# Program order for SyncE's DMA queue in layers 1 to 3 of a four-layer graph-attention kernel

## The chip, the cores and the metric

The kernel runs on one core of a Trainium2 chip. The metric is the device time of one execution in microseconds (us). The core's engines work side by side, each with its own list of instructions: TensorE (PE in the profile; PEld are its weight loads), VectorE (DVE), ScalarE (ACT), GpSimd (POOL) and SyncE (SP). In this kernel SyncE issues the plain transfers between the core's memories and DRAM, and POOL issues the indirect ones, which gather rows by index. A program writes its instructions once, in one sequence; a scheduler then gives each engine its order, and semaphores hold an instruction until what it needs is there.

## What is computed

Four graph-attention layers over 4096 nodes with 256 features, all with the same adjacency matrix (about one entry in 256 set, and the diagonal). Each ends in a residual and a layer norm:

```python
# layers 0 and 1: 4 heads of 64; layer 2: 2 heads of 128, separate weights for source, target and value
h   = x @ W
e   = leaky_relu(src[:, None] + dst[None, :], 0.2)     # one number per node on each side, per head
att = softmax(where(adj, e, -inf), axis=1)
x   = layernorm(x + att @ h)
# layer 3: one head, softmax of e and of -e, both over x, then a product and elu
hp  = concat([att(e) @ x, -att(-e) @ x], axis=1)
x   = layernorm(x + elu(hp @ fc_W))
```

In layer 2 the softmax runs over the other axis of a transposed score, which is the same form. `fc_W` is multiplied in ahead of the attention, so layer 3 gathers two blocks of 256 values per node.

## The kernel before

**Lists.** While layer 0 runs, the kernel turns the adjacency matrix into packed neighbour lists. The 4096 nodes are 32 row tiles of 128. For each row tile the columns that have an entry are packed into 13 groups (`NG`) of 128 gathered rows; with the tile's own 128 rows that makes 14 positions (`NP`). Groups 0 to 5 (`FRONT`) hold nodes of the first 17 row blocks (`MIX`) alone; groups 6 to 12 may hold any node. (A dense version stands behind a flag, for other matrices; it doesn't run here.)

**One row tile** (`RowTile`) has two halves of seven positions: half 0 is groups 0 to 5 and the own rows, half 1 is groups 6 to 12. `load` issues, for half 0, the edge terms `S` and the mask `mk` on SyncE; for half 1, the residual input `y` on SyncE; then for each position a gather `G` from the layer's `vals` on POOL (L629), or for the own rows a plain load `G` on SyncE (L626). `half` makes the attention weights `w` on ScalarE and VectorE (L670 and L666 to L671; in layer 3 L657 to L660) and multiplies them on PE (L679 in layer 1, L682 in layers 2 and 3). `finish` divides by the softmax's sum, adds `y` and normalizes (`norm`); the row goes to `xp` in DRAM, or in layer 3 to `out`.

**Projection of a finished row** (`Projection`): transpose (L532), copy `xT` on ScalarE (L537), products with the next layer's weights (L546), the row of `vals` on VectorE (L572), its store on SyncE (L574), then the edge terms (L578 to L585). So row m of the next layer's `vals` can exist a few steps after tile m of this layer is done. A gather of groups 0 to 5 of the next layer waits for `vals` rows 0 to 16, and one of groups 6 to 12 for all 32.

**Whole rows.** In layer 2 the last three blocks of four row tiles, and in layer 3 the last block, aren't gathered: `whole_rows` multiplies them densely, with loads of `Sw`, `mw` and `vw` on SyncE (L874, L886, L888) and products on PE (L911). These pieces are spread over the half steps of the other tiles.

**The order of the program.** A layer goes in half steps `part(m, 0)` and `part(m, 1)`. A part 0 first asks for the loads of tiles m and m + 1 that aren't yet asked for. Then come the half's products, the pieces of a projection of an earlier row, and the finish of tile m - 1. `close` goes from one layer to the next: it writes the rest of this layer's work, mixed with the first halves of tiles 0 and 1 of the next. In `norm` the store of a finished row stands right behind the last operation on it:

```python
        for i, (y, m) in enumerate(self.group):
            nc.vector.tensor_scalar(y, y, mv[:, i, 0:1], r[:, i:i + 1], op0=ALU.subtract, op1=ALU.mult)
            dst = self.prog.out if self.n == 3 else self.shared["x"][self.n + 1]
            nc.sync.dma_start(out=dst[m * P:(m + 1) * P, :], in_=y)          # L958
```

This written order isn't that of the queue: the scheduler may put a load far ahead of where it is written, once its buffer is free. Buffers are rotating pools: 4 of `S` and `mk`, 9 of `y`, 16 slots for `G` (a slot holds two positions in layers 1 and 2, one in layer 3) and 14 more for half 1 of layer 3.

Of the kernel before, what the change touches and what calls it, by code (L numbers as in the profile page):

```python
# [37 lines left out]
F32 = mybir.dt.float32  # L38
# [12 lines left out]
P = 128  # L51
# [78 lines left out]
def to_tiles(ap):  # L130
    return ap.rearrange("(t p) f -> p t f", p=P)
# [55 lines left out]
class Program:  # L187
# [24 lines left out]

    def weights(self, n):

        nc, ins, H = self.nc, self.ins, HEADS[n]
        V = F if n < 3 else 2 * F
        wext = self.wpool.tile([P, KT, 2 * F + 4 * H4], F32, name="wext")
        ablks, nats, brow = [], [], None
        if n < 2:
            nc.sync.dma_start(out=wext[:, :, :F], in_=to_tiles(ins[f"W{n}T"]))  # L220
            for k, a in enumerate(("src", "dst")):
                ablk = self.small.tile([P, KT, H4], F32, name=f"ablk{k}")
                nc.vector.memset(ablk, 0.0)
                for h in range(H4):
                    r = slice((h % 2) * D4, (h % 2) * D4 + D4)
                    vec = ins["a0s" if k == 0 else "a0d"][h] if n == 0 else ins["a1"][h, k * D4:(k + 1) * D4]
                    load_vec(nc, ablk[r, h // 2, h:h + 1], vec)
                ablks.append(ablk)
                nats.append(ins[f"W{n}"])
        elif n == 2:  # L230
            nc.sync.dma_start(out=wext[:, :, :F], in_=to_tiles(ins["W23T"]))
            for k in range(2):
                ablk = self.small.tile([P, KT, 2], F32, name=f"ablk{k}")
                nc.vector.memset(ablk, 0.0)
                for h in range(2):
                    load_vec(nc, ablk[:, h, h:h + 1], ins["a2"][h, k * P:(k + 1) * P])
                ablks.append(ablk)
                nats.append(ins["W21" if k == 0 else "W22"])
            brow = self.small.tile([1, F + 3 * H], F32, name="brow")
            nc.sync.dma_start(out=brow[:, :F], in_=ins["b23"].rearrange("(o f) -> o f", o=1))  # L240
            ones = self.small.tile([1, P], F32, name="ones")
            nc.vector.memset(ones, 1.0)
            self.ones = ones
        else:
            fc = to_tiles(ins["fc3"])
            for k in range(2):
                nc.sync.dma_start(out=wext[:, :, k * F:(k + 1) * F], in_=fc[:, k * KT:(k + 1) * KT, :])
                ablk = self.small.tile([P, KT, 1], F32, name=f"ablk{k}")
                for q in range(KT):
                    load_vec(nc, ablk[:, q, 0:1], ins["a3"][(k * KT + q) * P:(k * KT + q + 1) * P])  # L250
                ablks.append(ablk)
                nats.append(ins["W3T"])

        T = TERMS[n]

        def scaled(dst, src, k):

            nc.vector.tensor_scalar(dst[:, k * T:(k + 1) * T], src, SLOPE, None, op0=ALU.mult)
            if k == 1:
                nc.vector.tensor_scalar(dst[:, 2 * T:3 * T], src, NEG_SLOPE, None, op0=ALU.mult)  # L260
                if n == 3:
                    nc.vector.tensor_scalar(dst[:, 3 * T:4 * T], src, -NEG_SLOPE, None, op0=ALU.mult)

        for k in range(2):
            nat = self.io.tile([P, KT, F], F32, name="nat")
            nc.sync.dma_start(out=nat, in_=to_tiles(nats[k]))
            for m in range(KT):
                pw = self.bank(self.banks)
                for q in range(KT):
                    nc.tensor.matmul(pw[:, :T], nat[:, q, m * P:(m + 1) * P], ablks[k][:, q, :],  # L270
                                     start=(q == 0), stop=(q == KT - 1))
                scaled(wext[:, m, V:], pw[:, :T], k)
            if n == 2:
                bcol = self.small.tile([P, KT], F32, name=f"bcol{k}")
                for q in range(KT):
                    load_vec(nc, bcol[:, q:q + 1], ins["b21" if k == 0 else "b22"][q * P:(q + 1) * P])
                pb = self.bank(self.banks)
                for q in range(KT):
                    nc.tensor.matmul(pb[:1, :T], bcol[:, q:q + 1], ablks[k][:, q, :],
                                     start=(q == 0), stop=(q == KT - 1))  # L280
                scaled(brow[:, V:], pb[:1, :T], k)
        return wext, brow


    def lists(self, ctx):
# [191 lines left out]

    def run(self):
        ins, nc = self.ins, self.nc
        w0 = self.weights(0)  # L480
        layer = Layer(self, 0)
        with ExitStack() as ctx:
            lists = self.lists(ctx)
            xs = []
            for q in range(NT // 2):
                slot = self.g0.tile([P, 2 * ROW[0]], F32, name="G")
                nc.sync.dma_start(out=slot[:, :2 * F].rearrange("p (t f) -> p t f", t=2),
                                  in_=to_tiles(ins["x"][2 * q * P:2 * (q + 1) * P, :]))
                xs += [slot[:, :F], slot[:, F:2 * F]]

            line = [Projection(self, 0, w0, x, m, (self.ptwo[0], self.ptwo[1], self.pfour))
                    for m, x in enumerate(xs)]
            turns, listed = NT + 5, 0
            for m in range(turns):
                while listed < BT + LEAD and listed * turns <= m * (BT + LEAD):
                    next(lists)
                    listed += 1
                for k, step in enumerate(Projection.STEPS):
                    if 0 <= m - k < NT:
                        step(line[m - k])  # L500

            for m in range(NT):
                layer.part(m, 0)
                if m + LEAD < NT:
                    next(lists)
                layer.part(m, 1)
            for _ in lists:
                pass
        self.g1 = self.pool("g1", 14)
        self.bk, self.vp, self.dp = self.pool("bk", 1), self.pool("vp", 6), self.pool("dp", 8)  # L510
        self.mwp = self.pool("mwp", 2)
        for n in (1, 2, 3):
            following = Layer(self, n)
            layer.close(following)
            following.steps()
            layer = following
        layer.close(None)


class Projection:  # L520
# [184 lines left out]
class Layer:  # L705
# [3 lines left out]
    def __init__(self, prog, n):  # L709
        self.prog, self.n, self.nc, self.shared = prog, n, prog.nc, prog.shared  # L710
        self.count = NT - WHOLE[n] * BT
        self.tiles = {}
        self.loaded = set()
        self.units = self.whole_rows()
        self.total = WHOLE[n] * NT * (1 if n < 3 else 2)
        self.used = 0
        self.nxt = self.middle = self.stored = None
        self.group = []
        self.ready = []
        self.step = 0  # L720


# [21 lines left out]
    def part(self, m, part):  # L744


        if part == 0:
            if m == 2 and self.n < 3:
                self.set_banks()
                self.nxt = self.prog.weights(self.n + 1)  # L750
            for q in (m, m + 1):
                for half in range(2):
                    self.load(q, half)
        if WHOLE[self.n]:
            self.half_with_whole(m, part)
        else:
            self.half_alone(m, part)
# [63 lines left out]
    def close(self, following):  # L821

        last = self.count - 1
        self.step += 2
        if self.stored is not None:
            self.stored.store()
        if self.middle is not None:
# [28 lines left out]
        for _, y, m in self.ready:  # L856
            self.set_banks()
            Projection(self.prog, self.n + 1, self.nxt, y, m).all()
        if following is not None:
            for m in (1, 2):  # L860
                following.load(m, 0)
            following.tile(1).half(0)
            following.load(3, 0)
# [64 lines left out]
    def norm(self, y, m):  # L928
# [25 lines left out]
            nc.vector.tensor_tensor(r, r, u, op=ALU.mult)  # L954
        for i, (y, m) in enumerate(self.group):
            nc.vector.tensor_scalar(y, y, mv[:, i, 0:1], r[:, i:i + 1], op0=ALU.subtract, op1=ALU.mult)
            dst = self.prog.out if self.n == 3 else self.shared["x"][self.n + 1]
            nc.sync.dma_start(out=dst[m * P:(m + 1) * P, :], in_=y)  # L958
            if self.n < 3:
                self.ready.append((self.step + 1, y, m))  # L960
        self.group = []

    def positive(self, acc, whole=False):
# [5 lines left out]
        z = pool.tile([P, F], F32, name="zw", bufs=BT) if whole else pool.tile([P, F], F32, name="z")  # L969
        nc.scalar.activation(z, acc[:, :D], AF.Copy, scale=rec)  # L970
        return z

    def finish(self, m, acc, y, z):
        n, nc, ep = self.n, self.nc, self.prog.ep
# [483 lines left out]
```

## Time and profile before

| | before |
|---|---|
| time, median of 3 | 2342.57 us (2339.33 to 2343.09) |
| profiled execution, span | 2346.8 us, TensorE clock 0.95 |
| gathers of layer 1 on POOL | 812 to 1350 us |
| gathers of layer 2 | 1351 to 1779 us |
| gathers of layer 3 | 1812 to 2311 us |
| moved by gathers, by plain transfers | 245.30 MB, 243.42 MB |

Layer 0 and the lists take the first 800 us or so and aren't touched by the change. The profile gives, for each engine, its busy time and number of instructions; for each group of instructions, its busy time, the mean time of one and the idle time just before it with what ended it; and a table of waits names for each line what it waited for, with the total, the number of times and the longest. A share of busy time is a mean over the four layers, which have different limits.

### The profile page before, as it was taken

What the parts mean: (1) busy time and instruction counts of PE and PEld (TensorE: products, weight loads), DVE (VectorE), ACT (ScalarE), POOL (GpSimd) and SP (SyncE); (2) the same over time, 40 slices, a digit from 0 to 9 for tenths busy, and PEclk for the clock granted to TensorE, in tenths of its full rate; (3) what the DMA queues carried; (4) which work ended last, traced back from release to release, by engine and by line L of the source; (5) the groups of instructions that cost most, each with busy time, mean ns of one, the idle gap of its engine ahead of it and who ended that gap; (6) DMA issues with size and microseconds to landing.
All of it is one profiled execution on the core that took longest, in us unless ns stands there. A gap on an engine that the chain in (4) does not pass through costs nothing.

```text
span 2346.8 us, 49828 instructions
## 1 busy us (share of the span) xinstructions
PE 2052.4 (87%) x15689; PEld 1864.7 (79%) x15689; DVE 1838.1 (78%) x6100; ACT 1747.3 (74%) x5137; POOL 1582.6 (67%) x1596
## 2 busy tenths in 40 slices
PE   4878898989988769999999889889898799979996
PEld 3668788888888759988888879888887688868885
DVE  3889999999987759989899859876866365656567
ACT  4779898897787749988888859877663666666663
POOL 2127887777788757777777767755553677777773
PEclk7999999999999979999999989999999899989998
DMA  8889687775555556666666657666665788888883
GB/s 278 267 269 322 220 284 255 245 268 155 157 140 159 148 168 182 190 176 170 174 175 183 167 147 202 200 187 188 187 179 150 248 250 276 268 245 267 272 251 119
DMA packets 250325, 492.01 MB, mean 210 GB/s; under 512 B 44385, under 2 KB 156610, under 8 KB 249666
## 3 DMA queue, kind: packets, MB, share of 16 engines
q0 software_dynamic: 81536, 245.30, 37.1%
q1 hardware_dynamic: 168514, 243.42, 32.5%
q8 instruction: 126, 2.06, 0.4%
q14 instruction: 149, 1.22, 0.2%
HBM read 436.24 MB, written 52.31 MB: 208 GB/s over the span
## 4 chain that ended last, share of the span: by engine, by line
PE 47%; DVE 20%; DMA 18%; ACT 8%; issue 4%; POOL 3%; SPq 0%; ACTq 0%; DVEq 0%; POOLq 0%
PE bank L679 17%; PE bank L682 12%; DMA G<-vals,idx 12%; PE bank L911 7%; PE bank L546 5%; DVE w L671 5%; PE bank L436 4%; DMA G<-vals 3%; POOL G L629 3%; DVE w L666 3%; DVE w L667 3%; ACT w L670 3%; DVE oh L430 2%; DMA raw<-in_adjB_dram 2%; ACT pw L900 1%
## 5 line engine op out<-in xcount | busy, mean ns | idle before, releaser
L629 POOL DMA_INDIRECT G<-vals,idx x1456 | 1569.6, 1078 | 718.5 <-issue 188.1
L670 ACT ACTIVATE w<-S,G 128x128 f32<-128x128 f32 x3248 | 1009.6, 391 | 204.7 <-DMA G<-vals,idx 194.6
L679 PE MATMUL bank<-w,G 128*65 128x128 f32 x7168 | 846.8, 279 | 94.9 <-DVE w L667 65.0
L679 PEld LDWEIGHTS bank<-w,G 128*65 128x65 f32 x7168 | 810.4, 142 | 109.8 <-DVE w L667 84.5
L682 PE MATMUL bank<-G,w 128*128 128x257 f32 (+1 forms) x2688 | 499.4, 344 | 34.8 <-ACT z L970 11.5
L682 PEld LDWEIGHTS bank<-G,w 128*128 128x128 f32 x2688 | 439.2, 196 | 84.7 <-ACT z L970 13.9
L671 DVE SCALAR_TENSOR_TENSOR w<-w,mk 128x896 f32<-128x896 f32 x272 | 292.6, 1082 | 42.8 <-ACT w L670 42.1
L911 PE MATMUL bank<-vw,pw 128*128 128x129 f32 (+1 forms) x2048 | 304.8, 306 | 14.3 <-ACT zw L970 13.0
L911 PEld LDWEIGHTS bank<-vw,pw 128*128 128x128 f32 x2048 | 279.4, 195 | 32.0 <-ACT zw L970 13.4
L666 DVE TENSOR_SCALAR w<-S,G 128x128 f32<-128x128 f32 x896 | 238.7, 298 | 80.0 <-DMA G<-vals,idx 78.9
L657 ACT ACTIVATE w<-S,G 128x128 f32<-128x128 f32 x392 | 137.9, 389 | 146.6 <-DMA G<-vals 96.6
L546 PE MATMUL bank<-wext,xT 128*128 128x268 f32 (+3 forms) x640 | 188.3, 427 | 49.7 <-ACT xT L537 45.9
L430 DVE TENSOR_SCALAR oh<-iota,place 128x256 bf16<-128x256 f16 (+2 forms) x992 | 223.7, 298 | 8.3 <-PE bank L436 7.9
L671 DVE SCALAR_TENSOR_TENSOR w<-w,bank 128x896 f32<-128x896 f32 x192 | 206.0, 1078 | 8.9 <-ACT w L670 8.8
L436 PE MATMUL bank<-mk,oh 128*128 128x132 fp8e4 x2336 | 188.7, 228 | 15.7 <-DVE oh L430 8.7
L436 PEld LDWEIGHTS <-oh 128*128 128x128 bf16 x2336 | 147.3, 100 | 51.3 <-DVE oh L430 23.5
L546 PEld LDWEIGHTS bank<-wext,xT 128*128 128x128 f32 x640 | 122.0, 208 | 72.8 <-ACT xT L537 50.8
L908 DVE TENSOR_TENSOR pw<-pw,mw 128x512 f32<-128x512 f32 x64 | 43.9, 690 | 137.8 <-ACT pw L907 71.2
L901 DVE SCALAR_TENSOR_TENSOR pw<-pw,mw 128x512 f32<-128x512 f32 x192 | 127.8, 687 | 21.2 <-ACT pw L900 19.8
L373 ACT ACTIVATE mk<-raw 128x1024 uint8<-128x1024 int32 x128 | 131.5, 1063 | 16.9 <-DMA raw<-in_adjB_dram 16.5
L900 ACT ACTIVATE pw<-Sw,d 128x512 f32<-128x512 f32 x192 | 132.9, 708 | 3.4 <-PE bank L911 3.2
L443 ACT ACTIVATE cm<-bank 128x384 uint8<-128x384 f32 (+1 forms) x160 | 70.1, 451 | 60.4 <-PE bank L436 58.4
(131 smaller groups left out, 1710.5 us busy)
## 6 DMA issues: line engine op xcount, KB each, us to landing
raw<-in_adjB_dram SPq DMA_DIRECT2D x128, 512.0 KB
mk<-maskC SPq DMA_DIRECT2D x112, 224.0 KB
G<-vals,idx POOLq DMA_INDIRECT x1456
S<-edge SPq DMA_DIRECT2D x64, 256.0 KB
vw<-vals SPq DMA_DIRECT2D x96, 129.0 KB
xp<-y SPq DMA_DIRECT2D x96, 128.0 KB
y<-xp SPq DMA_DIRECT2D x96, 128.0 KB
mw<-maskW SPq DMA_DIRECT2D x20, 528.0 KB
```

Of the source, the lines that this page charges most:

```text
L430: nc.vector.tensor_scalar(oh[:, :n * P], iota[:, :n * P], self.place[:, it, j:j + 1], None, op0=ALU.is_equal)
L436: nc.tensor.matmul(accs[b][:, s * MC:(s + 1) * MC], oh[:, (k - a) * P:(k - a + 1) * P], mk[:, j, it, :].bitcast(FP8), start=touches[b][0] ...
L546: nc.tensor.matmul(pp[:, :c1 - c0], self.xT[:, k, :], wext[:, k, c0:c1], start=(k == 0), stop=(k == KT - 1 and brow is None))
L629: nc.gpsimd.indirect_dma_start(out=self.place(pos), out_offset=None, in_=sh["v"][n][:NODES[t], :], in_offset=bass.IndirectOffsetOnAxis(ap= ...
L657: nc.scalar.activation(w[0][:, k, :], S[:, 0, :], AF.Relu, bias=d(k, 0))
L666: nc.vector.tensor_scalar(w[h][:, k, :], S[:, h, :], d(k, h), LEAST, op0=ALU.mult, op1=ALU.max)
L670: nc.scalar.activation(w[h][:, k, :], S[:, h, :], AF.Exp, bias=d(k, h))
L671: nc.vector.scalar_tensor_tensor(w[h], w[h], LEAST, mh, op0=ALU.max, op1=ALU.mult)
L679: nc.tensor.matmul(accs[0][:Wd, h * P:(h + 1) * P], v, w[h][:, k, :], **how)
L682: nc.tensor.matmul(a, w[h][:, k, :], v, **how)
L900: nc.scalar.activation(p, S[:, h], AF.Exp, bias=d)
L911: nc.tensor.matmul(accs[it][:, c:c + Wd], p[:, it, :], v[:, c:c + Wd], start=(j == 0 and h == heads[0]), stop=(j == NT - 1), skip_group_ch ...
```

## The change

From the end of layer 0 on, SyncE is taken out of the scheduler's hands: its transfers are issued in the order in which the program writes them. So that this order is a good one, the program is changed in two places. A store of a finished row isn't written at once: `norm` notes the row, and `save` writes the stores in the next half step, behind the loads of the next row tile. And `weights`, which loads the next layer's weights and multiplies them, is split at a `yield`, so that its loads stand at m = 1 and the products that use them at m = 2. The aim is that a load never stands behind a store that still waits for its row. The arithmetic is the same.

```diff
--- before.py
+++ after.py
@@ -261,9 +262,18 @@
                 if n == 3:
                     nc.vector.tensor_scalar(dst[:, 3 * T:4 * T], src, -NEG_SLOPE, None, op0=ALU.mult)
 
+        loaded, bcols = [], []
         for k in range(2):
             nat = self.io.tile([P, KT, F], F32, name="nat")
             nc.sync.dma_start(out=nat, in_=to_tiles(nats[k]))
+            loaded.append(nat)
+            if n == 2:
+                bcol = self.small.tile([P, KT], F32, name=f"bcol{k}")
+                for q in range(KT):
+                    load_vec(nc, bcol[:, q:q + 1], ins["b21" if k == 0 else "b22"][q * P:(q + 1) * P])
+                bcols.append(bcol)
+        yield None
+        for k, nat in enumerate(loaded):
             for m in range(KT):
                 pw = self.bank(self.banks)
                 for q in range(KT):
@@ -271,15 +281,12 @@
                                      start=(q == 0), stop=(q == KT - 1))
                 scaled(wext[:, m, V:], pw[:, :T], k)
             if n == 2:
-                bcol = self.small.tile([P, KT], F32, name=f"bcol{k}")
-                for q in range(KT):
-                    load_vec(nc, bcol[:, q:q + 1], ins["b21" if k == 0 else "b22"][q * P:(q + 1) * P])
                 pb = self.bank(self.banks)
                 for q in range(KT):
-                    nc.tensor.matmul(pb[:1, :T], bcol[:, q:q + 1], ablks[k][:, q, :],
+                    nc.tensor.matmul(pb[:1, :T], bcols[k][:, q:q + 1], ablks[k][:, q, :],
                                      start=(q == 0), stop=(q == KT - 1))
                 scaled(brow[:, V:], pb[:1, :T], k)
-        return wext, brow
+        yield wext, brow
 
 
     def lists(self, ctx):
@@ -477,7 +484,7 @@
 
     def run(self):
         ins, nc = self.ins, self.nc
-        w0 = self.weights(0)
+        _, w0 = self.weights(0)
         layer = Layer(self, 0)
         with ExitStack() as ctx:
             lists = self.lists(ctx)
@@ -509,12 +516,13 @@
         self.g1 = self.pool("g1", 14)
         self.bk, self.vp, self.dp = self.pool("bk", 1), self.pool("vp", 6), self.pool("dp", 8)
         self.mwp = self.pool("mwp", 2)
-        for n in (1, 2, 3):
-            following = Layer(self, n)
-            layer.close(following)
-            following.steps()
-            layer = following
-        layer.close(None)
+        with self.tc.manual_schedule(engines={mybir.EngineType.SP}):
+            for n in (1, 2, 3):
+                following = Layer(self, n)
+                layer.close(following)
+                following.steps()
+                layer = following
+            layer.close(None)
 
 
 class Projection:
@@ -716,7 +724,7 @@
         self.used = 0
         self.nxt = self.middle = self.stored = None
         self.group = []
-        self.ready = []
+        self.ready, self.unsaved = [], []
         self.step = 0
 
 
@@ -745,12 +753,16 @@
 
 
         if part == 0:
+            if m == 1 and self.n < 3:
+                self.coming = self.prog.weights(self.n + 1)
+                next(self.coming)
             if m == 2 and self.n < 3:
                 self.set_banks()
-                self.nxt = self.prog.weights(self.n + 1)
+                self.nxt = next(self.coming)
             for q in (m, m + 1):
                 for half in range(2):
                     self.load(q, half)
+        self.save()
         if WHOLE[self.n]:
             self.half_with_whole(m, part)
         else:
@@ -822,6 +834,7 @@
 
         last = self.count - 1
         self.step += 2
+        self.save()
         if self.stored is not None:
             self.stored.store()
         if self.middle is not None:
@@ -856,6 +869,7 @@
         for _, y, m in self.ready:
             self.set_banks()
             Projection(self.prog, self.n + 1, self.nxt, y, m).all()
+        self.save()
         if following is not None:
             for m in (1, 2):
                 following.load(m, 0)
@@ -954,8 +968,7 @@
             nc.vector.tensor_tensor(r, r, u, op=ALU.mult)
         for i, (y, m) in enumerate(self.group):
             nc.vector.tensor_scalar(y, y, mv[:, i, 0:1], r[:, i:i + 1], op0=ALU.subtract, op1=ALU.mult)
-            dst = self.prog.out if self.n == 3 else self.shared["x"][self.n + 1]
-            nc.sync.dma_start(out=dst[m * P:(m + 1) * P, :], in_=y)
+            self.unsaved.append((m, y))
             if self.n < 3:
                 self.ready.append((self.step + 1, y, m))
         self.group = []
@@ -969,6 +982,13 @@
         z = pool.tile([P, F], F32, name="zw", bufs=BT) if whole else pool.tile([P, F], F32, name="z")
         nc.scalar.activation(z, acc[:, :D], AF.Copy, scale=rec)
         return z
+
+    def save(self):
+
+        dst = self.prog.out if self.n == 3 else self.shared["x"][self.n + 1]
+        for m, y in self.unsaved:
+            self.nc.sync.dma_start(out=dst[m * P:(m + 1) * P, :], in_=y)
+        self.unsaved = []
 
     def finish(self, m, acc, y, z):
         n, nc, ep = self.n, self.nc, self.prog.ep
```

## The prediction, made before the changed kernel ran

> **What bounds the kernel now.** I read the page first, for how full each engine is, then cut the run by layer, and in each layer asked which engine never waits.
>
> ```profile
> PE 2052.4 (87%) x15689; PEld 1864.7 (79%) x15689; DVE 1838.1 (78%) x6100; ACT 1747.3 (74%) x5137; POOL 1582.6 (67%) x1596
> PE 47%; DVE 20%; DMA 18%; ACT 8%; issue 4%; POOL 3%; SPq 0%; ACTq 0%; DVEq 0%; POOLq 0%
> L629 POOL DMA_INDIRECT G<-vals,idx x1456 | 1569.6, 1078 | 718.5 <-issue 188.1
> L546 PE MATMUL bank<-wext,xT 128*128 128x268 f32 (+3 forms) x640 | 188.3, 427 | 49.7 <-ACT xT L537 45.9
> ```
>
> TensorE looks like the bound, at 87%, and SyncE's queue (SPq), which the change reorders, has 0% of the chain that ended last. The cut by layer says more. These are the windows of the steady parts of layers 1, 2 and 3 (length; busy time of PE, PEld, DVE, ACT, POOL; clock; DMA share; GB/s):
>
> ```profile
> 890.00:1340.00 450.00, 421.09 (x3546) 394.52 (x3545) 415.40 (x1336) 391.04 (x1312) 340.90 (x359) 0.98 0.65 177
> 1400.00:1770.00 370.00, 332.29 (x2648) 319.98 (x2649) 282.88 (x872) 276.42 (x744) 237.24 (x222) 0.96 0.67 191
> 1900.00:2300.00 400.00, 376.85 (x1701) 326.83 (x1699) 232.07 (x689) 254.18 (x542) 304.30 (x297) 0.97 0.85 263
> ```
>
> Each gather on POOL is followed by 0.30 us that no busy time covers. Layer 1: 340.9 + 359 x 0.30 = 448.6 of 450 us, so POOL never rests there. Layer 3: 304.3 + 297 x 0.30 = 393.4 of 400, nearly the same, with PE close behind (376.9). Layer 2: 237.2 + 222 x 0.30 = 303.8 of 370: POOL has slack, and PE works 332 us. The waits of POOL, layer 1 and then layer 2, agree (total us, times, longest):
>
> ```profile
> POOL G L629 <- issue: 37.5, 123, 0.3
> POOL G L629 <- PE bank L679: 37.2, 122, 0.3
> ```
> ```profile
> POOL G L629 <- ACT w L670: 48.0, 31, 9.8
> POOL G L629 <- issue: 42.5, 126, 2.4
> ```
>
> No wait in layer 1 is longer than the gap. So a layer ends when its gathers end (1 and 3) or when PE's list ends (2), and what counts is when each layer's gathers may begin. POOL's timeline shows a stop at each boundary, where the first gather over all 32 row blocks waits for the last `vals` row (start, length, and in brackets the idle time before):
>
> ```profile
> 858.10 0.94 POOL L629 DMA_INDIRECT G<-vals,idx  x1 [14.76 <-DMA ablk<-in_a_dram]
> ...
> 1390.25 1.08 POOL L629 DMA_INDIRECT G<-vals,idx  x1 [7.70 <-DMA vals<-row]
> ...
> 1845.48 0.94 POOL L629 DMA_INDIRECT G<-vals,idx  x1 [5.75 <-issue]
> ```
>
> I call these moments the gates. (The transfer named in the first bracket landed at the same moment; the row itself went out at 855.44.) The queue's own fault shows in layer 3, in SyncE's waits and in ScalarE's waits from 1900 to 2310:
>
> ```profile
> SPq L958 <- DVE y L956: 226.8, 80, 13.0
> ```
> ```profile
> ACT w L657 <- DMA G<-vals: 96.6, 20, 7.2
> ```
>
> SyncE stands 226.8 us before stores of finished rows, and behind them stands the own-row load `G` (L626). In SyncE's timeline the store went at 2205.39 and `G` at 2205.83; ScalarE got it at 2209.88 after 3.80 us idle.
>
> [...] the last layer 2 row was issued at 1387.33 and POOL went on at 1390.25. [...]
>
> **The change part by part.**
>
> *Loads first, in steady state.* `G` of tile m+1 goes ahead of the stores, a half step or more earlier, so ScalarE's 96.6 us should vanish. But POOL has only 400 - 393.4 = 6.6 us to give in that window, so nearly all of the 96.6 us is slack. I count the one stop of POOL there that isn't a gap (5.57 us at tile 15, about 2093, behind ScalarE) and 2 us for ScalarE's lag after the last gathers (the last half's first relu starts 3.8 us after its last gather was issued): -7.6 us. In layer 1 `G` lands 20 us or more before use: nothing. `S`, `mk` and `y` lose prefetch depth (`S` from about 40 us ahead to one tile, 16 us or so); a load lands in 2 to 7 us, so VectorE and ScalarE don't see it.
>
> *Boundary 0 to 1.* Two things move. The gate: before, `S` and `G` of tile 0 are loaded early, so the first halves of tiles 0 and 1 (ScalarE, 819.3 to 837.3) come between rows 28 and 31, whose stores go at 826.75, 839.50, 849.29 and 855.44. After, those loads stand behind the rows, so the second of these halves (9.1 us) no longer delays the last row: gate 858.1 - 9.1 = 849.0. And the order of the gathers: comparing the two instruction orders, before has 24 gathers ahead of the gate (groups 0 to 5 of tiles 0 to 3), after only 12 (tiles 0 and 1); the other 12 stand behind the first gather that needs all rows. 12 x 1.25 = 15.0 us of work moves from idle time into the saturated part. Layer 1 ends 15.0 - 9.1 = +5.9 us later.
>
> *Boundary 1 to 2.* The same exchange: 12 instead of 24 ahead of the gate. The last rows run together instead of around one first half (14 products of 0.344 us, 4.8 us) and 13 products of whole rows, of which I take 0.7: the gate comes 5.5 us earlier relative to the end of layer 1, so +0.4. POOL is then 15.4 us late. The first products of the second halves wait for it[...]; whole-row products move around them (24 before and 48 after tile 0's second half, 72 by tile 2 as before) but the sum is the same. Between tile 1's last exponential (1412.7) and tile 2's first (1416.7) are 4 us of slack: +11 at the end of layer 2. PE has little idle time later to win it back (29.9 us, all behind the transposed row L537).
>
> *Boundary 2 to 3.* Here the order turns the other way: before has 20 gathers ahead of the gate, after 12. The first of them started at 1811.63. Before, rows 17, 18 and 19 are stored at 1812.44, 1822.97 and 1839.14, the last one behind the first half of tile 0 on PE. After, PE runs these rows together; at some 5 us each they land 15 us after 1811.6, as the 12 gathers end (12 x 1.25 = 15). So no stop: -5.45 (5.75 less the gap), and -3.2 for two short stops at tiles 2 and 3. 44 whole-row products (0.306 us each, 13.5 us) leave the hole at the boundary for the steady part, where PE has 23 us idle in 400; I take them as hidden, bounded by 0 and 8.
>
> *The end.* Loads of tile 27 now stand behind the four `out` stores of the whole block; `G` of tile 26 no longer waits. I put these against each other: 0, bounded by -3 and +4. Splitting `weights()` moves 1 or 2 us of loads, beside other work: 0.
>
> Sum: +11 - 5.45 - 3.2 - 7.6 = -5.2 us, 2342.6 - 5.2 = 2337.4; I say 2337.
>
> **The rivals.**
> - *The lost head start costs more than layer 3 returns.* Were the first gate only 4 us earlier, layer 1 would end +11, and layer 2 +16; with the tile 15 stop still there (+5.6) and 5 us of deferred products on the path: 2337.4 + 5 + 5.6 + 5 = 2353. For it: POOL in layer 1 has no slack, and PE has little in layer 2. Against it: the rows really are freed of the halves that sat between them.
> - *The queue was the brake.* If the first gate comes as early as 842 (16 us, both halves gone), layer 1 ends -1 and layer 2 +4, and layer 3 is as forecast: 2330; if the deferred gathers of layer 2 are also hidden by whole-row work, 2323. For it: ScalarE's 96.6 us[...]. Against it: POOL is full in two of the three layers.
> - *No change*, with the sum near zero: each term is uncertain by some 4 us.
>
> **How the numbers follow.** Forecast case (2330 to 2344) 0.5, lost head start 0.28, brake 0.22. The bounds of the forecast case lie on both sides of -0.2% (2337.9): about half of it is faster, most of the rest within. Faster 0.25 + 0.21 = 0.46; slower 0.28 + 0.04 = 0.32; within 0.22. The range, 2318 to 2358, takes in the two rivals' values and leaves a tenth on each side.
>
> **What would show it.** In the changed kernel's trace: 12 gathers, then a stop, and the gate near 849; POOL without stops to some 1356; gate 2 near 1390, then 12 gathers of tiles 2 and 3 before tile 0's second half; no stop of POOL at tile 0 of layer 3; ScalarE's wait for `G<-vals` gone, POOL still full. The forecast is wrong if the first gate isn't earlier, if layer 2 ends where it did, if layer 3's gathers take less than 1.25 us each (then POOL wasn't the bound), or if new waits for `S`, `mk` or `y` show on VectorE or ScalarE.

## The result and the profile after

The changed kernel takes 2377.11 us (median of 4, 2368.34 to 2380.65), the kernel before, run beside it, 2340.95. The ratio is 1.0149 (95% interval 1.0119 to 1.0180): 36 us slower, where 2337 was forecast with a range up to 2358. The intervals of this document leave out two executions, one each of e10 and e11, in a slow state at 10.6 and 11.5 ms.

The changed kernel's lines are numbered differently: the gather L629 is now L637, `S` L619 is L627, the own-row load L626 is L634, the stores L958 are L990, and the weights L657 and L670 are L665 and L678. First the page of the changed kernel:

```profile
PE 2052.4 (86%) x15689; PEld 1866.0 (79%) x15689; DVE 1846.4 (78%) x6100; ACT 1760.5 (74%) x5137; POOL 1599.3 (67%) x1596
L637 POOL DMA_INDIRECT G<-vals,idx x1456 | 1586.2, 1089 | 728.1 <-issue 186.1
L554 PE MATMUL bank<-wext,xT 128*128 128x268 f32 (+3 forms) x640 | 182.8, 416 | 31.6 <-ACT xT L545 25.7
```

PE does the work it did before (2052.4 us both times); POOL's busy time grew by 16.7 us and the others' by 1.3 to 13.2. So on PE the loss is idle time, and the page doesn't say where. The windows of the steady parts of layers 1, 2 and 3, shifted to where they now lie:

```profile
903.00:1353.00 450.00, 421.32 (x3551) 394.12 (x3549) 415.52 (x1336) 389.19 (x1300) 341.24 (x358) 0.98 0.62 174
1445.00:1815.00 370.00, 335.75 (x2693) 323.64 (x2691) 291.76 (x986) 269.32 (x729) 239.84 (x214) 0.97 0.65 189
1928.00:2328.00 400.00, 385.19 (x1764) 336.48 (x1762) 248.38 (x742) 278.93 (x573) 308.90 (x298) 0.99 0.86 269
```

Layer 1 runs at its old rate: 358 gathers in 450 us, 359 before. So its loss lies ahead of its steady part. In layer 2 POOL makes 214 gathers in 370 us, where it made 222; but the window of before began in the busy stretch behind the gate, and one that begins as far behind tile 1 as the new one (1416 to 1786) has 217. In layer 3 PE is now at 385 of 400 us. POOL's timeline at the three gates:

```profile
852.58 0.94 POOL L637 DMA_INDIRECT G<-vals,idx  x1 [20.95 <-DMA vals<-row]
...
1399.26 0.94 POOL L637 DMA_INDIRECT G<-vals,idx  x1 [20.36 <-DMA vals<-row]
...
1856.31 0.94 POOL L637 DMA_INDIRECT G<-vals,idx  x1 [4.53 <-issue]
```

The stops at the first two gates grew from 14.76 and 7.70 us to 20.95 and 20.36. And in ScalarE's waits, the first line from layer 3 (1928 to 2338), the second from layer 2 (1450 to 1825):

```profile
ACT w L665 <- DMA G<-vals,idx: 106.5, 110, 4.0
```
```profile
ACT w L678 <- DMA S<-edge: 45.7, 14, 6.0
```

The 96.6 us of waiting for the own rows in layer 3 are gone as forecast, and in their place ScalarE waits as long for the gathers (19.9 us before): they were slack. The 45.7 us for `S` are new; in the kernel before layer 2 has no such line. But there too a wait went: before, from 1420 to 1790, ScalarE waited 77.0 us for gathers, and that line is gone.

To place the loss, I cut each profiled execution at eight marks that stand in every trace: the first gather of layer 1, the last exponential of tile 1 and of layer 1's last tile, the same two in layer 2, the last relu of tile 1 and of the last tile in layer 3, and the end. These marks, but for the first and the end, stand on ScalarE. The last three rows cut the same executions on POOL, each layer from its first gather to the next layer's first, and layer 3 to the end. Times in us; e13 to e17 are experiments told below.

| stretch | before | changed | e13 | e14 | e16 | e17 |
|---|---|---|---|---|---|---|
| to layer 1's first gather | 812.4 | 815.9 | 815.8 | 820.4 | 817.2 | 811.5 |
| layer 1, start (tiles 0 and 1) | 69.5 | 77.5 | 62.8 | 78.0 | 62.5 | 78.0 |
| layer 1, rest | 475.6 | 476.4 | 478.7 | 477.3 | 478.8 | 475.0 |
| layer 2, start | 55.3 | 71.7 | 57.9 | 73.3 | 56.5 | 73.0 |
| layer 2, rest | 369.1 | 381.4 | 382.2 | 369.3 | 371.0 | 383.8 |
| layer 3, start | 91.6 | 70.5 | 67.9 | 69.6 | 71.9 | 86.9 |
| layer 3, rest | 445.5 | 456.6 | 453.6 | 460.5 | 453.7 | 447.1 |
| end | 27.9 | 24.9 | 25.1 | 25.4 | 25.4 | 25.6 |
| span | 2346.8 | 2375.0 | 2343.8 | 2373.8 | 2337.0 | 2380.9 |
| by gathers: layer 1 | 538.2 | 548.1 | 535.7 | 549.3 | 535.8 | 546.6 |
| by gathers: layer 2 | 461.0 | 473.1 | 460.9 | 462.8 | 450.0 | 477.6 |
| by gathers: layer 3 and end | 535.2 | 537.8 | 531.4 | 541.3 | 534.1 | 545.2 |

The column of changes (after less before) reads +3.5, +8.0, +0.8, +16.4, +12.3, -21.1, +11.1 and -3.0, in all +28.2. (The profiled execution before took 2348.6 us, longer than any of the timed ones, so this is less than the 36 us between the medians.) The first row varies by 9 us among the changed kernel, e14 and e17, whose programs are the same up to there, so I read nothing from it.

The changes from the rest of layer 2 on can't be read as they stand. At layer 2's last exponential PE still has 18.3 us to go to that layer's last product before the change (it ends at 1800.2), and 4.4 us after (1827.3). So some 14 us that look lost in the rest of layer 2 and won at the start of layer 3 are only a shift of ScalarE against PE. In the windows between the two marks of the rest of layer 2, before and after, PE is busy 328.1 of 369.1 us and 346.0 of 381.4:

```profile
1412.74:1781.87 369.13, 328.09 (x2623) 315.27 (x2622) 284.95 (x915) 276.72 (x751) 234.54 (x219) 0.97 0.67 189
1441.51:1822.95 381.44, 345.99 (x2763) 333.54 (x2762) 299.96 (x1006) 279.37 (x759) 242.41 (x217) 0.96 0.64 186
```

The stretch is 12.3 us longer because 17.9 us more of PE's work lies in it; PE stands idle 35.4 us there, and 41.0 before. In the start of layer 2 it is the other way: PE's idle time grew from 9.9 to 30.9 us. The changes by gathers are +3.5 up to layer 1, +9.9 in layer 1, +12.1 in layer 2 and +2.7 in layer 3; cut at PE's last product of the gathered tiles of layers 1 and 2 instead they are +3.5, +6.8, +16.8 and +1.0. Both cuts say the same: the loss is made in layers 1 and 2, and layer 3 gave nothing back.

### The profile page after: what moved, and what is told of

Read it like the earlier page. It is cut to its first block, busy times and chain, and to the rows that moved or that the text cites. A ratio compares the mean times of both kernels' runs of the same rounds, so it can differ in the third digit from the quotient of the medians.

```text
span 2375.0 us, 49553 instructions
## 1 busy us (share of the span) xinstructions
PE 2052.4 (86%) x15689; PEld 1866.0 (79%) x15689; DVE 1846.4 (78%) x6100; ACT 1760.5 (74%) x5137; POOL 1599.3 (67%) x1596
## 5 line engine op out<-in xcount | busy, mean ns | idle before, releaser
L637 POOL DMA_INDIRECT G<-vals,idx x1456 | 1586.2, 1089 | 728.1 <-issue 186.1
L678 ACT ACTIVATE w<-S,G 128x128 f32<-128x128 f32 x3248 | 1000.4, 392 | 176.0 <-DMA G<-vals,idx 112.9
L665 ACT ACTIVATE w<-S,G 128x128 f32<-128x128 f32 x392 | 139.4, 392 | 146.6 <-DMA G<-vals,idx 130.9
L554 PE MATMUL bank<-wext,xT 128*128 128x268 f32 (+3 forms) x640 | 182.8, 416 | 31.6 <-ACT xT L545 25.7
L443 PE MATMUL bank<-mk,oh 128*128 128x132 fp8e4 x2336 | 189.1, 228 | 18.9 <-DVE oh L437 13.3
L667 DVE TENSOR_TENSOR w<-w,mk 128x896 f32<-128x896 f32 x56 | 61.3, 1094 | 114.0 <-ACT w L666 110.4
L380 ACT ACTIVATE mk<-raw 128x1024 uint8<-128x1024 int32 x128 | 131.5, 1064 | 18.5 <-DMA raw<-in_adjB_dram 18.3
```

What stands on the lines that cost most here:

```text
L443: nc.tensor.matmul(accs[b][:, s * MC:(s + 1) * MC], oh[:, (k - a) * P:(k - a + 1) * P], mk[:, j, it, :].bitcast(FP8), start=touches[b][0] ...
L554: nc.tensor.matmul(pp[:, :c1 - c0], self.xT[:, k, :], wext[:, k, c0:c1], start=(k == 0), stop=(k == KT - 1 and brow is None))
L637: nc.gpsimd.indirect_dma_start(out=self.place(pos), out_offset=None, in_=sh["v"][n][:NODES[t], :], in_offset=bass.IndirectOffsetOnAxis(ap= ...
L665: nc.scalar.activation(w[0][:, k, :], S[:, 0, :], AF.Relu, bias=d(k, 0))
L678: nc.scalar.activation(w[h][:, k, :], S[:, h, :], AF.Exp, bias=d(k, h))
```

## The experiments

Two theories. H, the lost head start: at the boundaries 0 to 1 and 1 to 2 twelve gathers fell behind the gate. Q, later loads: in program order `S`, `mk` and `y` come too late in the steady parts.

Runs e1 to e12 fell on chips on which the kernel before took 2841 (e1 to e4), 2899 (e5 to e8) and 2898 us (e9 to e12), at a mean TensorE clock of 0.87, 0.86 and 0.86; e13 to e18 on chips where it took 2344 to 2347 at 0.95, as on the first. The first kind is called the slower chips below, though nothing shows that the chip is the cause. Each ratio is to the kernel before, run beside it. On the slower chips POOL doesn't bound layer 1: from 1130 to 1730 in e1, 344 gathers take 327.8 + 344 x 0.30 = 431 of 600 us. PE, at a clock of 0.82 there (0.98 in the kernel before, from 890 to 1340), is the fullest engine with 498.2 of 600 us. So H has less to take there. One trace of each run is kept, and on these chips the rest of layer 1 varies from 643 to 695 us among them.

**The parts of the change, one at a time.** Program order off, and then on with immediate stores:

```diff
-        with self.tc.manual_schedule(engines={mybir.EngineType.SP}):      # e1
+        if True:
```

> The changed kernel without the program order: SyncE's queue is the scheduler's again; the delayed stores and the split weights stay. Its gathers stand in the order of the kernel before (24 ahead of the first and second gate, 20 ahead of the third). Theory H (lost head start: the 12 gathers that fell behind the gate at the boundaries 0 to 1 and 1 to 2 make the loss) expects 2341, within 6 us of the kernel before, with the layer 1 gathers ending near 1350. Theory Q (later loads: the new program order starves VectorE and ScalarE of S and mk in the steady parts) expects the same here, 2341. If the delayed stores or the split weights cost by themselves, it is over 2350.

Measured: 0.9984 (0.9940 to 1.0029). The delayed stores and the split weights cost nothing that shows by themselves. It doesn't tell H from Q.

```diff
             self.unsaved.append((m, y))                                   # e2
+            self.save()
```

> The changed kernel with the program order kept, but each store written straight behind the norm, as before. Built so, its gathers stand in the order of the kernel before (24 ahead of the first two gates). Theory H expects most of the loss gone: 2335 to 2352, layer 1's gathers ending between 1340 and 1355. Theory Q expects it at least as slow as the changed kernel, 2375 or more, since SyncE's queue is in program order and now stands before the stores ahead of the loads.

Measured: 1.0298 (1.0257 to 1.0339), as Q said and not as H said. With 24 gathers ahead of the gate the start of layer 2 takes 63.3 us (in e1 52.1; in e5, the changed kernel on such a chip, 85.0), but the rest of layer 2 takes 467.6 (403.2) and that of layer 3 540.8 (491.5). ScalarE's waits from 1820 on show why:

```profile
ACT w L665 <- DMA S<-edge: 137.9, 21, 14.4
ACT w L678 <- DMA S<-edge: 39.2, 8, 16.1
```

SyncE stood 422.1 us (44 times) before stores of finished rows in this run, with loads behind them in program order, and ScalarE waited 177.1 us in these two lines for `S`; in e1 it has no such wait. So H can't be all.

**Layers alone.** The context is put around single layers (e4: the end of layer 2 and layer 3; e9: the end of layer 0 and layer 1; e10: layers 1 and 2):

```diff
+            with (self.tc.manual_schedule(engines={mybir.EngineType.SP}) if n in (3,) else ExitStack()):
```

> Program order from the end of layer 2 on only; layers 1 and 2 as the scheduler puts them. Theory H expects layers 1 and 2 as before and layer 3 as in the changed kernel, where it took 2.7 us more than before: 2344, between 2338 and 2349. Theory Q, with the loss spread over the steady parts, expects about a third of the 36 us: 2353.

> Program order from the end of layer 0 to the end of layer 1 only. Theory H: where POOL bounds layer 1 (a chip like the first), +10 to +13 us, ratio 1.0045 to 1.0055; where PE bounds it (a chip with a slower TensorE), under 5 us. Theory Q: no change on either, since no wait for S stands in layer 1.

> Program order in layers 1 and 2, layer 3 as the scheduler puts it: the complement of the run with layer 3 only. Both theories: the whole loss of the changed kernel, ratio 1.012 to 1.018, since layer 3 alone made no difference. Of it, theory H puts 15 to 25 us between the end of layer 1 and tile 1's second half in layer 2, theory Q puts 10 to 20 us between that and the end of layer 2.

Measured: layer 3 alone 1.0009 (0.9984 to 1.0033), layer 1 alone 1.0003 (0.9984 to 1.0023), layers 1 and 2 together 1.0096 (1.0062 to 1.0130). On chips of this kind most of the loss is layer 2's. Layer 3's no change is as H expected (its 2.7 us are the cut by gathers), and the 16.3 us that the prediction counted on in layer 3 would be a ratio of 0.994, outside the interval; layer 1's no change fits both. In e10 the start of layer 2 takes 82.0 us (e9, where it isn't in program order: 50.6), and the rest 421.3 (406.0): both theories' places show, though layer 3's start is 14.9 us shorter here than in e9, so part of this is the shift of ScalarE again. 1.0096 is less than both had expected.

**POOL in program order too.**

```diff
-        with self.tc.manual_schedule(engines={mybir.EngineType.SP}):
+        with self.tc.manual_schedule(engines={mybir.EngineType.SP, mybir.EngineType.Pool}):
```

> The changed kernel with POOL's gathers in program order too, which puts the 24 gathers ahead of all three gates. Theory H expects layer 1 to end 10 to 15 us earlier than in the changed kernel (1363 there) and layer 2's second halves 20 to 28 us earlier, with 2345 to 2356 in all; the third gate's good order is lost, which gives back 5 to 10. Theory Q expects 2370 to 2380.

Measured: 1.0070 (1.0047 to 1.0093), about half the changed kernel's loss gone. In us the expectation was for a chip like the first, so only the ratio counts: 2345 to 2356 is 1.002 to 1.006. Other things move with the order (the rest of layer 2 takes 403.2 us, as in e1, for which neither theory has a reason), so this isn't a clean test.

**The two causes, each undone by itself.** First the changed kernel again, as a measure on the slower chips:

> The changed kernel once more, as the measure for the three beside it. On a chip like the first both theories expect 2377, 1.5% above the kernel before. On one whose TensorE is slower, so that PE and not POOL is the bound, theory H (the 12 gathers behind the gate make the loss) expects a smaller share, under 1.2%; theory Q (the new order starves VectorE and ScalarE of S) gives no number for it.

Measured: 1.0149 (1.0088 to 1.0210), more than H's bound of 1.2% though the interval reaches under it. Then gathers first, an edit in `close`:

```diff
         if following is not None:
-            following.load(0, 0)
+            for m in range(3 if self.n < 2 else 1):      # e13: range(3) at all three boundaries
+                following.load(m, 0)
```

> The changed kernel with one edit: at the boundaries 0 to 1 and 1 to 2 the half 0 loads of tiles 1 and 2 are written ahead of the last rows, next to those of tile 0. Built so, 24 gathers stand ahead of the first two gates again; the third keeps the changed kernel's order. Theory H: layer 1's gathers end about 10 us earlier than in the changed kernel and the second halves of layer 2's tiles 0 and 1 some 20 us earlier; about 2355 where the changed kernel has 2377, that is a ratio to it of 0.991. Theory Q: no change against the changed kernel, within 5 us, since S, mk and y are loaded as late as there in the steady parts.

> The gathers-first version again, for a chip on which POOL bounds layer 1. There theory H expects layer 1 and the start of layer 2 to give back 20 to 25 us of the changed kernel's 36: ratio to the kernel before 1.004 to 1.008. On a chip with a slower TensorE as before: 1.012.

Measured: 1.0121 (1.0085 to 1.0157) and, on another slow chip, 1.0056 (1.0028 to 1.0084); the two don't agree well. In e6 the starts of layers 1 and 2 fall from 93.1 and 85.0 us (e5) to 81.4 and 63.4, which is H's sign, but the rest of layer 1, where POOL isn't the bound on such a chip (431 of 600 us in e1), takes 688.0 instead of 680.2. The total alone settles nothing; the same edit where POOL is the bound does:

> Gathers first at all three boundaries, loads in the steady parts as in the changed kernel. Theory H alone: on a chip like the first 1.002 to 1.007; on a slower one 1.005 to 1.010. If S in the steady parts costs as much (Q), the version with all edits beside it is 10 us or more faster than this one.

Measured: 1.0015 (0.9999 to 1.0030), against the changed kernel's 1.0149, and the starts of layers 1 and 2 are shorter by 14.7 and 13.8 us (table); by gathers, layers 1 and 2 are shorter by 12.4 and 12.2. POOL's timeline of e13 at the first two gates:

```profile
845.70 0.94 POOL L637 DMA_INDIRECT G<-vals,idx  x1 [0.30 <-DMA vals<-row]
855.48 0.94 POOL L637 DMA_INDIRECT G<-vals,idx  x1 [8.84 <-DMA xp<-y]
...
1387.49 0.94 POOL L637 DMA_INDIRECT G<-vals,idx  x1 [4.61 <-DMA vals<-row]
```

The gates stand some 3 us later and 12 us earlier than in the changed kernel, but what counts is that POOL comes to them with 24 gathers done. Twelve gathers at 1.25 us are 15.0 us; 14.7 and 13.8 were got back. H is shown, with one reserve: the edit moves `S`, `mk` and the own rows of these tiles along with their gathers. It acts at the third gate too, and layer 3 is 6.4 us shorter by gathers, with no stop of POOL at that gate. The prediction took it as given, with no trace that shows it, that a gather stopped at a gate stops the ready ones behind it. Here it is seen: in the changed kernel twelve gathers that need no more than row 16 stand 20.95 us behind the stopped one, and in e13 they are done before it.

Then `S` a half step earlier, an edit in `part` (e7 in all layers, e14 in layer 2 only; `mk`, the own rows and six gathers of the tile go with it):

```diff
                 for half in range(2):
                     self.load(q, half)
+        elif self.n == 2:                                # e7: else:
+            self.load(m + 2, 0)
         self.save()
```

> The changed kernel with the half 0 loads of tile m+2 written at part 1 of tile m, a half step earlier; the gathers' order at the gates is that of the changed kernel. Theory Q: ScalarE's waits for S in layer 2 (about 50 us) go, and with them 15 us or more. Theory H: those waits lie beside PE's own work, so within 5 us of the changed kernel.

> The changed kernel with S, mk and G loaded a half step earlier in layer 2 only. Theory Q places the late S in layer 2: the time between tile 1's second half and the end of layer 2 falls by 12 us or more, and the whole by as much, as with the prefetch in all layers (ratio 1.010 to 1.013 on a slow chip). If the prefetch worked through layers 1 or 3, the ratio stays at 1.015.

Measured: e7 1.0117 (1.0063 to 1.0172), with the rest of layer 2 at 402.2 us against 425.1 in e5. And e14 1.0069 (1.0045 to 1.0094): the rest of layer 2 takes 369.3 us, as before the change, instead of 381.4, and no other row down to the end moves by more than 5 (two of them, longer, hide the gain in this trace's span, its slowest execution). By gathers layer 2 is 10.3 us shorter, and PE's idle time in its rest falls from 35.4 to 24.7. So `S` late is a real cost in layer 2, 10 to 12 us that an earlier load gets back. It is not what sets the changed kernel's layer 2 apart from the one before: there PE stood idle 41.0 us in the same stretch with `S` in time, 32.2 of it (1420 to 1790) for the row copy `xT`, a wait that fell to 17.5 (1450 to 1825). The mechanism is seen on SyncE and ScalarE. The changed kernel, tile 4 of layer 2, SyncE's timeline and then ScalarE's:

```profile
1472.14 0.32 SPq L582 DMA_DIRECT2D vals<-row  x1
1472.51 0.42 SPq L627 DMA_DIRECT2D S<-edge  x1
```
```profile
1477.02 1.28 ACT L678 ACTIVATE w<-S,G 128x128 f32<-128x128 f32 x4 [1.80 <-DMA S<-edge]
```

`S` is issued 0.37 us behind the store of a row that SyncE had to wait for, and ScalarE starts as it lands. `save` doesn't help here: it delays the stores of finished rows (L990), and this is the store of a projected row (L582). In the kernel before, the same tile's `S` was issued at 1401.92 and used at 1445.70. From tile 4 on `S` was issued 44 to 73 us before its use, and in the changed kernel 4 to 8 us, so that ScalarE often starts as it lands. SyncE's wait behind this, from 1450 to 1825:

```profile
SPq L582 <- DVE row L580: 75.6, 21, 10.1
```

The kernel before has nearly the same wait (65.8 us from 1420 to 1790), but no needed `S` behind it. The half step doesn't restore the old lead: in e14 `S` is used 3 to 11 us after its issue, and ScalarE still waits 24.8 us for it (45.7 without the edit). It is enough that `S` is issued earlier.

Both edits together:

> Both edits, gathers first and S a half step earlier. Theory H: as with the gathers first alone, within 5 us. Theory Q: as with the prefetch alone.

> Gathers first at all three boundaries and S a half step earlier. With both causes at work this is the version that should not lose: ratio 0.996 to 1.003 on either kind of chip. If layer 3's good order mattered, it is 5 to 10 us slower than the version with both edits that kept it.

> The version with all edits on another chip: 0.993 to 0.998 again on a chip with a slower TensorE; on one like the first, where POOL bounds layers 1 and 3, 0.994 to 1.002.

Measured: e8 1.0012 (0.9982 to 1.0042), where each theory alone had expected no more than one edit gives; e12, with the gathers first at the third gate too, 0.9955 (0.9937 to 0.9973); and the same kernel on a chip like the first (e16) 0.9941 (0.9922 to 0.9959), 2330.05 against 2343.69 us. This version beats both kernels, and e13 by 15.5 us, as Q said. In e16 layer 2 is 23.1 us shorter by gathers than in the changed kernel, about what e13 and e14 give together (12.2 and 10.3). On the slower chips it doesn't add up so: the rest of layer 2 takes 415.4 us in e8 and 421.5 in e12, where e7 has 402.2 and e11, without the prefetch, 422.4. Why is open. The third gate's good order, which e8 has and e12 doesn't, brought nothing that shows: e12 isn't slower.

**What the delayed stores are worth.** The version with all edits, but stores straight behind the norm as in e2:

> All edits, but each store again straight behind the norm. With S loaded a half step earlier the stores stand ahead of fewer needed loads: if the delay is what makes the program order bearable, this is 1.010 or more above the kernel before; if the prefetch does the same work, it is within 0.3% of the version with all edits.

Measured: 1.0237 (1.0192 to 1.0282), against 0.9941 with the delay: some 69 us of 2344. The prefetch doesn't do the same work; the rest of layer 2 takes 424.2 us (e16: 371.0). SyncE's wait for a finished row in the whole run is 750.2 us here and 542.0 in e16:

```profile
SPq L994 <- DVE y L973: 750.2, 86, 19.0
```
```profile
SPq L993 <- DVE y L973: 542.0, 69, 14.2
```

Both are far more than the 226.8 us of the kernel before (the changed kernel has 499.5). What a queue waits says little; what stands behind the wait says more.

**Layer 3.** By ScalarE's marks its start is 21.1 us shorter in the changed kernel and its rest 11.1 longer. The suspicion was the whole-row products that had left the hole at the boundary. In e17 eight steps (32 products) of them are put back on the changed kernel, in e18 on the version with all edits:

```diff
             self.tile(last).finish()
             if following is not None:
+                following.begin(8)          # runs the first 8 steps of whole_rows
                 following.tile(0).half(0)
```

> The changed kernel with one edit: the first 8 steps of layer 3's whole rows (32 products) are written in the close of layer 2, ahead of the first half of tile 0, so that PE has them in the hole. If the deferred products make layer 3's loss, the time from tile 1's second half to tile 27's falls from 457 us (before: 446) to 450 or less, and the ratio from 1.015 to 1.012 or less. If not (the loss lies in the transfers or the clock), both stay within 3 us.

> The version with all edits, and the same 8 steps of whole rows in the hole. If the deferred products cost there too: 0.990 to 0.993, against 0.994 without. If they delay the last rows instead, 0.996 or more.

Measured: e17 1.0173 (1.0153 to 1.0193), e18 1.0014 (0.9996 to 1.0031). The rest of layer 3 fell to 447.1 us as expected, but the start rose from 70.5 to 86.9, and the total rose. POOL's third gate in e17:

```profile
1872.91 1.21 POOL L637 DMA_INDIRECT G<-vals,idx  x1 [22.49 <-issue]
```

The stop there is 22.49 us instead of 4.53. The last `vals` row went out 33.5 us after the first gather of layer 3, in the changed kernel 16.1. So the products in the hole hold up the rows that the gate waits for, and moving them out is the smaller price: 9.5 us paid in the rest for 16.4 at the start; by gathers layer 3 is 7.4 us longer with them.

## Why the prediction was wrong, step by step

The same sum, step by step (us; the prediction's terms, and the change in the trace by gathers):

| | said | measured |
|---|---|---|
| up to layer 1's first gather | 0 | +3.5 |
| layer 1 | +5.9 | +9.9 |
| layer 2 | +5.1 | +12.1 |
| layer 3 and the end | -16.3 | +2.7 |
| in all | -5.2 | +28.2 |

- *POOL bounds layers 1 and 3*: right. Layer 1's rest took 476.4 us for 475.6, and layer 3 from its first to its last gather 500.2 for 499.3.
- *Boundary 0 to 1*: right. The gate came 9.0 us earlier measured from the first gather of layer 1 (36.7 us after it, 45.7 before); 9.1 was said. The order cost 14.7 (e13; 12.4 by gathers); 15.0 was said. POOL's stop grew by 6.2, 5.9 was said; the rest of the 9.9 are short stops behind it, 2.37 us the longest.
- *Boundary 1 to 2*: the mechanism was right, the size wrong. The gate came 3.3 us earlier measured from the end of layer 1's weights (32.8 to 29.5), not 5.5. The order cost 13.8 by e13. From the gate to tile 1's last exponential it took 42.2 us, before 22.5, so 4.8 more than the 15.0 of the twelve gathers. And the 4 us of slack between tiles 1 and 2 absorbed nearly nothing: 3.6 us before (1413.12 to 1416.70), 3.0 after (1441.90 to 1444.87). About 5 us of the way from gate to exponential stay in e13, with the gathers first (27.6); what makes them wasn't tried, but by tile 2's first exponential they are gone (58.8 us after layer 1's last, before 59.3, in the changed kernel 75.1).
- *`S` loses depth, and ScalarE doesn't see it*: this step failed. I took the program's distance, "one tile, 16 us or so", for the time that is left; 4 to 8 us were left. ScalarE has the weights of the next tile ahead of the end of a row that the program writes before them, and SyncE hasn't: in program order `S` of tile m+1 waits behind the store of a row that ScalarE has already gone past (tile 4 of layer 2: store at 1472.14, `S` at 1472.51, ScalarE idle 1.80 us for it). It cost 10 to 12 us in layer 2 (e14), for nothing said. The changed order gave more than that back there in other waits (PE's idle time fell from 41.0 to 35.4 us), so this cost doesn't show when the two kernels are compared. In layer 1's steady part (903 to 1353) no such wait stands; ahead of it ScalarE waits 7.4 us for `S` and VectorE 7.8.
- *Loads first in layer 3* (-7.6): the wait for `G` went, and the waiting moved to the gathers, as argued. The stop at tile 15 went too (5.81 us at 2088.72 in the trace; the prediction has 5.57 at about 2093). But a new one of 6.57 us stands at 1909.51, behind PE's products, the gathers of the layer are busy 378.5 us for 374.7, and from the last gather to the end it takes 37.7 us for 35.8. The fault was also read too large: the 226.8 us that SyncE stands before stores are the whole run's, and 82.6 of them lie from 1790 on.
- *Boundary 2 to 3* (-8.7): this step failed. Of its two terms the stop at the gate was to go, because the last rows would follow each other at some 5 us. They went out 7.1 and 7.8 us apart (1838.26, 1845.40, 1853.21), and POOL stood 4.53 us at the gate, before 5.75. The order with only 12 gathers ahead of it wasn't the better one either: with 24 (e13) there is no stop. The short stops did shrink, by some 3 us. *The deferred whole-row products*, taken as hidden and bounded by 8, were no net cost: put back, they make layer 3 longer (e17).

Of the 33.4 us between the sum and the trace, layer 3's return, which never came, makes 18.9, layer 2 7.0, layer 1 4.0, and 3.5 come before the first gather, where I can't tell them from scatter. So the step that failed most is the gain of layer 3: stops were counted as gained one by one, and others took their place. Cut on PE, layer 3's share is 17.3 and layer 2's 11.7. Why the new stop and the longer gathers come wasn't tried. The rival of the lost head start (2353) came nearest: it had layer 1 ending 11 us later and layer 2 16, where 9.9 and 22.0 were measured, and had layer 3 returning less, though for a stop at tile 15 that did go. Of the signs named, two speak against the forecast: POOL still stops at the third gate, and new waits for `S` show on ScalarE.

## What to carry to other kernels

When one engine's queue is taken from a scheduler, look for two things: what the other queues' orders become (here 12 gathers that had filled a hole fell behind the gate, 12 to 15 us at each of two boundaries), and how far the engines that use the loads run ahead of the program; a load in program order was only early where it stood before every instruction whose inputs come later than its use (`S` of layer 2, 0.37 us behind a store that waited, was issued 4 to 8 us before its use; in the scheduler's order 44 to 73). Delay the stores, write the loads that fill a hole before the work that makes the hole, and write the other loads a half step earlier: with all three the program order is 0.6% faster than the scheduler's, with the first alone 1.5% slower. A stop that goes isn't a gain until the layer's end comes earlier (the 5.81 us at tile 15 went, and layer 3 took 2.7 us more by gathers). And a layer's length depends on the engine whose marks cut it: ScalarE's marks put some 14 us of these runs into the wrong layer. Filling a hole with other work wasn't free where the hole's end waits for a chain on the same engine (e17: POOL's stop at the third gate 22.49 us instead of 4.53).

## What the runs showed of the hardware that was not expected

The kernel before took 2341, 2841, 2899, 2898, 2344 and 2347 us on the six occasions, each within 1.5%, at a mean clock of about 0.95 or of 0.86 to 0.87. In layer 1's steady part the clock is 0.98 in the kernel before (890 to 1340) and 0.82 in e1 (1130 to 1730), a factor of 1.20, while the rest of layer 1 takes 674.1 us in e1 for 475.6, a factor of 1.42. In the same windows a gather comes every 1.74 us instead of every 1.25 (344 in 600 us, 359 in 450), a factor of 1.39. So the clock alone doesn't make it: in e1's window neither PE (498.2 of 600 us) nor POOL (431) is full. What makes these occasions slower isn't known, nor that it is the chip: the record has chip number 3 for 2899 and for 2344. It bears on experiments: a loss on POOL that is 12 to 15 us where POOL is the bound (448.6 of 450 us) didn't show in the total on such an occasion (e9, 1.0003).
